# A two-layer graph network on one core: the batch steps of the first layer in groups of their own, and fifteen copied tiles in fourteen groups

## The chip, the cores and the metric

The kernel runs on one core of one Trainium2 chip. The metric is the device time of one execution in microseconds, lower is better. The core has five engines that run side by side: PE (TensorE, matmuls and transposes), DVE (VectorE), ACT (ScalarE), POOL (GpSimd, here the issuer of gathers) and SP (SyncE, the issuer of plain DMAs). Each works through its own instructions in order; a semaphore makes one wait for another.

## The reference

12,500 nodes with 128 features, 200,000 edges sorted by their target `dst`, and 50 features for each edge. Two layers follow each other:

```python
h = relu(layernorm(x))
x = x + segment_sum(h[src], dst) @ W_rel.T + b_rel + h @ W_root.T        # layer 0
h = relu(layernorm(x))
edge = silu(edge_attr_50 @ We1 + be1) @ We2 + be2
agg = segment_sum(h[src] * edge, dst)
x = x + h + silu(agg @ Wn1 + bn1) @ Wn2 + bn2                            # layer 1
```

All of it is in float32.

## The kernel before

**Tiling.** The edges are cut into 196 groups of 1024, each of eight tiles of 128 edges. The nodes are cut into 25 batches of 512 (the last is smaller). For each layer a hand-written loop goes over the groups, and an edge tile goes through three steps: `fetch` gathers the 128 source rows into a buffer `hs` with an indirect DMA that POOL issues; `compare` (DVE) makes a 0/1 matrix `oh` that says which of 128 neighbouring target nodes each edge belongs to; `scatter` (PE, L391) multiplies the two and so sums the rows by target. `add` (DVE, L409) adds the result of a group to the sums of all nodes, which stay on the chip, transposed, in one half of the tensor `both`. There are six `hs` buffers, so POOL may gather up to six groups ahead of `scatter`.

**Layer 0's first 17 groups** normalise the gathered rows of `x` themselves; meanwhile all nodes are normalised once (`node_first`), written to memory as `h0_d`, and kept on the chip, transposed, in the other half of `both` (the table). From group 17 on the rows come from `h0_d`, already normalised.

**Copied tiles.** With all nodes in the table, a tile's rows can also be had without POOL: for each of its 128 edges a column of the table is copied into a tile `hc`, which PE transposes (`turn`, L633) and ACT puts into its place in `hs` (`place`, L639). The columns are shared between DVE (`HC[layer]` of them, L606) and ACT (the rest, L608). Their addresses come from a row of indices, `help_at`, that the engine's sequencer loads into registers (`take`, L591), at most `HL` = 16 at a time. `HELP[layer]` says how many tiles are copied in how many groups: layer 0 has (1, 1), one tile in each group, from group 18 on; layer 1 has (9, 10). A copied tile is the last of its group, and `fetch` leaves it out. `chunks` cuts a tile's columns over the groups that share the work, and `spread` issues those of one group after all else of that group. A tile is wanted `HW` = 4 groups after the group that ends its copying.

**Batch steps.** Edges are sorted, so the sums of a batch of nodes are complete after a known group (`ready[b]`). Then the batch is finished by a list of parts, which `plan` hangs to the groups that follow, one part for each. In layer 0 these are `node_sum` (PE: bias and two products, L471 and L475; then DVE at once: add the old features, L483, and the moments of the layer norm, L289 and L292; then ACT at once: the square root, L294), `node_norm` (DVE: reciprocal and scale, L299 and L301; ACT: the normalised rows, L308), `node_keep` (DVE, L512), `node_store` (SP: `h1_d` and `keep_d` to memory, and the load for the batch four later), `node_turn` (PE, four transposes, L531) and `node_send` (ACT, L537). All use one PSUM bank, `b3`, so that a batch's sum waits for the batch before to be sent. What falls beyond the last group is issued at its end. Layer 1's gathers wait until the last batches of `h1_d` are in memory.

**Order.** In each group of layer 0 the loop issues: the gathers of the next group (POOL), the next `compare` and the `add` of the group before (DVE), `scatter` (PE), then the planned parts of the group, then the columns (DVE and ACT). Engines run ahead of each other only as far as the semaphores let them.

Of the kernel before, what the change touches and what calls it, by code (L numbers as in the profile page):

```python
# [19 lines left out]
P = 128  # L20
D = 128
GT = 8
GE = GT * P
# [4 lines left out]
HB = 6  # L28
# [3 lines left out]
XB = 4  # L32
FB = 4
EP = 51
HELP = ((1, 1), (9, 10))
HC = (60, 56)
HW = 4
TABLE = 16512
HL = 16
# [27 lines left out]
def helped(n_nodes, n_edges):  # L67

    ng = n_edges // GE
    nbt = len(last_groups(n_nodes, n_edges))
    layers = []
    for begin, (tiles, groups) in ((min(ng, -(-nbt // 2) + FB) + 1, HELP[0]), (1, HELP[1])):
        ends = (begin - 1 - -(i + 1) * groups // tiles for i in range(ng * tiles // groups))
        layers.append((begin, [(e + HW, e) for e in ends if e + HW < ng - 1]))
    return layers


# [21 lines left out]
def kernel(  # L102
# [35 lines left out]
    NG = NT // GT  # L138
# [4 lines left out]
    batches = [(b * NB * P, min(NB, -(-(N - b * NB * P) // P))) for b in range(NBT)]  # L143
    FG = min(NG, -(-NBT // 2) + FB)
    places, blocks = help_places(N, n_edges)
    helps = [
        (layer, h, e, begin, j)
        for layer, (begin, groups) in enumerate(helped(N, n_edges))
        for j, (h, e) in enumerate(groups)
    ]  # L150
    helped_groups = {(layer, h) for layer, h, *_ in helps}

    def rows_of(ap, n0, rows, nt):
        return ap[n0 : n0 + rows * nt, :].rearrange("(t p) d -> p t d", p=rows)
# [36 lines left out]
    with (  # L191
# [9 lines left out]
        hs = many(HB, [P, GT, D], "hs")  # L201
# [8 lines left out]
        stn, mvn = many(3, [P, NB, 6], "stn"), many(3, [P, NB, 2], "mvn")  # L210
# [6 lines left out]
        h1 = h0[:2]  # L217
# [16 lines left out]
        def inc(ins, sem, by=1):  # L234

            if sem not in sems:
                sems[sem], counts[sem] = tc.alloc_semaphore(f"s_{sem}"), 0
            ins.then_inc(sems[sem], by)
            counts[sem] += by
            return sem, counts[sem]  # L240

        def at(engine, *needs):

            best = {}
            for need_ in needs:
                if need_ is not None:
                    best[need_[0]] = max(best.get(need_[0], 0), need_[1])
            for sem, n in best.items():
                if n > seen.get((engine.engine, sem), 0):
                    seen[engine.engine, sem] = n  # L250
                    engine.wait_ge(sems[sem], n)
# [4 lines left out]
        def fetch(layer, g):  # L256

            k = layer * NG + g
            at(G, done["src", 0 if g < 8 else 1], done.get(("ap", k - (HB if g < NG - 8 else LB))))
            if layer:  # L260
                at(G, *(done["h1 out", b] for b in range(max(0, NBT - 2), NBT)))
            elif g >= FG:
                at(G, *(done["h0 out", b] for b in range(max(0, NBT - 3), NBT)))
            for t in range(tiles_of[g] - ((layer, g) in helped_groups)):
                ins = G.indirect_dma_start(  # L265
                    out=hs[k % HB][:, t, :], out_offset=None,
                    in_=h1_d if layer else x if g < FG else h0_d,
                    in_offset=bass.IndirectOffsetOnAxis(
                        ap=src_sb[:, g * GT + t : g * GT + t + 1], axis=0
                    ),  # L270
                )
                done["hs", k] = inc(ins, f"hs{k % HB}", 16)
# [9 lines left out]
                ALU.is_equal,  # L282
            )

        def stats(xr, n, rows, st_, mv_, sd_, free):

            at(V, *free)
            for t in range(n):
                ins = V.bn_stats(st_[:rows, t, :], xr[:rows, t, :])  # L289
            at(V, inc(ins, "dve"))  # L290
            for t in range(n):
                ins = V.bn_aggr(mv_[:rows, t, :], st_[:rows, t, :])  # L292
            at(A, inc(ins, "dve"))
            ins = A.activation(sd_[:rows, :n], mv_[:rows, :n, 1], AF.Sqrt, bias=eps[:rows])  # L294
            return inc(ins, "act")

        def scales(n, rows, mv_, sd_, rs_, nm_, deviations):
            at(V, deviations)
            ins = V.reciprocal(rs_[:rows, :n], sd_[:rows, :n])  # L299
            at(V, inc(ins, "dve"))  # L300
            ins = V.scalar_tensor_tensor(  # L301
                nm_[:rows, :n], mv_[:rows, :n, 0], -1.0, rs_[:rows, :n], op0=ALU.mult, op1=ALU.mult
            )
            return inc(ins, "dve")
# [155 lines left out]
        def node_table(b, turned):  # L460
# [3 lines left out]
            ins = A.copy(halves[0][:, n0 : n0 + m], turned.rearrange("p t d -> p (t d)")[:, :m])  # L464
            done["table", b] = inc(ins, "act")

        def node_sum(b):

            n0, nt = batches[b]
            at(T, done.get(("sent", b - 1)), done["const"], done["ones"], done["table", b])  # L470
            T.matmul(op[:, :nt, :], ones_r, b_rel_r[:, :nt, :], start=True, stop=False)  # L471
            for half, w_sb in zip(halves, (w_root_sb, w_rel_sb)):
                for t in range(nt):
                    s = n0 + t * P
                    ins = T.matmul(  # L475
                        op[:, t, :], half[:, s : s + P], w_sb,
                        start=False, stop=(half is agg and t == nt - 1),
                    )
                at(T, done["add", ready[b]])
            done["op", b] = inc(ins, "pe")  # L480
            at(V, done["op", b], done["xt", b])
            o = op[:, :nt, :]
            ins = V.tensor_add(o, o, xt[b % XB][:, :nt, :])  # L483
            done["dev", b] = stats(
                op, nt, P, stn[2], mvn[2], sdn[2], (inc(ins, "dve"), done.get(("h1", b - 1)))
            )
            if b >= cleared:
                at(V, done["op", b], *done.get("columns", ()))
                ins = V.memset(halves[0][:, n0 : n0 + WG], 0.0)
                done["sums", 1].append(inc(ins, "dve"))  # L490

        def clear(b0, b1):
# [3 lines left out]
            ins = A.copy(halves[0][:, s0:s1], zero.to_broadcast([P, s1 - s0]))  # L496
            done["sums", 1].append(inc(ins, "act"))

        def node_norm(b):
            n0, nt = batches[b]  # L500
            at(A, scales(nt, P, mvn[2], sdn[2], rsn[2], nmn[2], done["dev", b]))
            if b < 2:
                at(A, *(done["h0 out", b] for b in range(max(0, NBT - 3), NBT)))
            else:
                at(A, done["h1 out", b - 2], done["keep", b - 2], done["h1 turned", b - 2])
            done["h1", b] = normalized(h1[b % 2], op, nt, P, rsn[2], nmn[2])
# [125 lines left out]
            at(T, done["b3"] if layer else done.get(("placed", i - 2)), done["table", NBT - 1])  # L632
            done["tile", i] = inc(T.transpose(bank, hc[i % 3], ident), "pe")  # L633

        def place(i, layer, h):
            bank = b3[:, :P] if layer else tp[i % 2][:, 0, :]
            k = layer * NG + h
            at(A, done["tile", i], done.get(("ap", k - HB)))
            done["hx", k] = done["placed", i] = inc(A.copy(hs[k % HB][:, GT - 1, :], bank), "act")  # L639
            if layer:  # L640
                done["b3"] = done["placed", i]

        with tc.tile_critical():
# [88 lines left out]
            def plan(layer, g, what):  # L732
                beside[layer].setdefault(min(max(g, 0), NG), []).append(what)

            cleared = NBT
            for layer, parts in (
                (0, (node_sum, node_norm, node_keep, node_store, node_turn, node_send)),
                (1, (node_hidden, node_out, node_out_store)),
            ):
                begin = 0 if layer else FG  # L740
                for b in range(NBT):
                    begin = max(begin, ready[b] + 1)
                    if not layer and begin > NG - 6:
                        cleared = min(cleared, b)
                    for i, part in enumerate(parts):
                        plan(layer, begin + i, lambda b=b, part=part: part(b))
                    begin += len(parts) - 1
            for i in range(4):
                b0, b1 = (cleared * j // 4 for j in (i, i + 1))
                if b0 < b1:  # L750
# [2 lines left out]
                plan(0, -(-NBT // 2) + 1, lambda b=b: node_load(b))  # L753
            for b in range(min(2, NBT)):
                plan(1, ready[0] - 1, lambda b=b: node_load(b, keep_d))
            for i, (layer, h, e, begin, j) in enumerate(helps):
                tiles, groups = HELP[layer]
                for g in range(begin, e + 1):
                    lo, hi = (min(max((g + d - begin) * tiles / groups - j, 0), 1) for d in (0, 1))
                    if lo < hi:  # L760
                        shares.setdefault((layer, g), []).append((i, lo, hi))
                plan(layer, e + 1, lambda i=i, layer=layer: turn(i, layer))
                if not layer:
                    plan(0, e + 2, lambda i=i, h=h: place(i, 0, h))
            placed = {e + 1: (i, 1, h) for i, (layer, h, e, *_) in enumerate(helps) if layer}
            plan(0, FG, check_a)
            plan(0, FG + 1, check_b)
            for g in range(0, min(2 * EG, NG), EG):
# [5 lines left out]
            for layer in range(2):  # L774
# [5 lines left out]
                for g in range(NG):  # L780
# [29 lines left out]
                        what()  # L810
                    spread(layer, g)
                    if layer and g in placed:
                        place(*placed[g])
                add(layer, NG - 1)
                for what in beside[layer].get(NG, ()):
                    what()
# [191 lines left out]
```

## Time and profile before

| | us |
|---|---|
| median of 3 runs (lowest to highest) | 4920.62 (4913.62 to 4926.87) |
| the profiled execution | 4865.67 |
| its span in the profile | 4863.9 |

Busy time by stage, from the windows of the trace:

| stretch, us | what runs | PE | DVE | ACT | POOL | PE clock |
|---|---|---|---|---|---|---|
| 0 to 275 | layer 0 without copied tiles | 94.7 | 120.7 | 133.4 | 177.2 | 0.75 |
| 275 to 2345 | layer 0 with copied tiles | 750.8 | 1129.1 | 1340.6 | 1125.3 | 0.61 |
| 2345 to 2450 | end of layer 0, start of layer 1 | 41.2 | 16.9 | 17.4 | 63.1 | 0.62 |
| 2450 to 4863 | layer 1 | 1668.0 | 1484.1 | 1559.7 | 1263.5 | 0.74 |

The busiest groups of the whole span (the page's fifth part) are POOL's gathers (2648 of 944 ns, 2499.4 us), ACT's column copies at L608 (23,936 of 190 ns, 2596.6 us in all since neighbours overlap), DVE's at L606 (19,840 of 150 ns, 1588.2 us) and PE's products at L391 (1268.7 us). The register loads at L591 take 1025 ns on ACT's sequencer and 1104 ns on DVE's in the median; they are not counted as busy.

How to read it: times are from one execution under the hardware profiler. In the lists of groups, the numbers after the bar are the busy time of the group, the mean of one instruction, and the idle time of the engine just before the group's instructions with what ended it; "issue" is idle time in which the engine waited for nothing that the profile shows, and "remote" one whose releaser is not known. Register, branch and semaphore instructions are not counted as busy.

### The profile page before, as it was taken

The numbers are of one execution on the slowest core, as the hardware profiler recorded it, in microseconds if no ns is written. First come the engines' busy times: TensorE is split into PE (matmuls) and PEld (weight loads), VectorE is DVE, ScalarE is ACT, GpSimd is POOL, SyncE is SP. The second block draws the span as 40 slices with busy tenths as digits, with TensorE's granted clock in tenths as the row PEclk, the third lists the DMA queues.
The fourth block names the chain that finished last, engine by engine and source line by source line (L and its number), as shares of the span: only waits on it lengthen the run. The fifth ranks groups of instructions, "written<-read, shape, count | busy, mean of one in ns | idle before, by whom it ended". The sixth has DMA issues, their size and how long they took to land.

```text
span 4863.9 us, 77667 instructions
## 1 busy us (share of the span) xinstructions
PE 2554.6 (53%) x11440; PEld 1986.8 (41%) x11440; DVE 2750.9 (57%) x21943; ACT 3051.0 (63%) x24975; POOL 2629.1 (54%) x2791
## 2 busy tenths in 40 slices
PE   2433333333333333334456767677666776667777
PEld 1423333332332333333344545455444554444555
DVE  3545555555455555555256566666655665666665
ACT  4646656666666666667356666666666666666664
POOL 6655555555555555554555455555554555555544
PEclk9666655566556666656677777777777777777778
DMA  3411111111111111111122222212221222222221
GB/s 109 112 49 50 51 43 47 47 52 46 44 45 53 45 45 53 47 47 43 52 63 58 59 62 63 59 55 61 64 58 55 59 61 59 63 61 61 58 57 48
DMA packets 187106, 275.72 MB, mean 57 GB/s; under 512 B 48331, under 2 KB 136658, under 8 KB 181586
## 3 DMA queue, kind: packets, MB, share of 16 engines
q0 software_dynamic: 89088, 182.63, 14.5%
q1 hardware_dynamic: 97300, 87.96, 5.9%
q14 instruction: 429, 3.51, 0.2%
q8 instruction: 93, 1.52, 0.1%
q10 hardware_dynamic: 196, 0.09, 0.0%
HBM read 244.89 MB, written 25.60 MB: 56 GB/s over the span
## 4 chain that ended last, share of the span: by engine, by line
ACT 33%; issue 28%; DVE 16%; PE 11%; another core or an unknown queue 8%; ACTq 3%; DVEq 1%; SPq 0%; DMA 0%
ACT hc L608 28%; DVE hc L606 9%; PE bank L391 4%; ACT hid L358 3%; PE pair L355 3%; ACTq L591 3%; DVE oh L278 2%; PE pair L368 2%; DVEq L591 1%; DVE stn L289 1%; ACT hs L639 1%; PE bank L475 1%; DVE st L289 0%; DVE hs L380 0%
## 5 line engine op out<-in xcount | busy, mean ns | idle before, releaser
L265 POOL DMA_INDIRECT hs<-h_d,src_sb x2648 | 2499.4, 944 | 2137.2 <-PE bank L391 1119.3
L608 ACT COPY hc<-both 128x4 uint8 x23936 | 2596.6, 190 | 1364.9 <-issue 1344.9
L606 DVE TENSOR_TENSOR hc<-both,bank 128x4 uint8<-128x4 uint8 x19840 | 1588.2, 150 | 1238.9 <-issue 1226.3
L391 PE MATMUL bank<-oh,hs 128*128 128x128 f32 x6252 | 1268.7, 386 | 291.1 <-issue 120.1
L391 PEld LDWEIGHTS bank<-oh,hs 128*128 128x128 f32 x6252 | 1194.4, 294 | 525.5 <-issue 264.2
L633 PE MATMUL pair<-ident,hc 128*128 128x128 f32 x172 | 73.0, 424 | 1281.1 <-ACT hc L608 411.5
L355 PE MATMUL pair<-ef,we_sb 50*128 50x512 f32 (+1 forms) x782 | 549.8, 837 | 75.8 <-ACT hid L358 33.5
L633 PEld LDWEIGHTS pair<-ident,hc 128*128 128x128 f32 x172 | 30.4, 176 | 1318.9 <-issue 778.5
L278 DVE TENSOR_TENSOR oh<-bank,rel 128x1024 f32<-128x1024 f32 x392 | 475.0, 1212 | 16.9 <-issue 16.7
L376 DVE TENSOR_TENSOR pair<-pair,be_sb 128x1024 f32<-128x1024 f32 x196 | 240.3, 1226 | 407.6 <-PE pair L368 214.9
L368 PE MATMUL pair<-we_sb,hid 128*128 128x128 f32 x3126 | 441.6, 302 | 4.7 <-issue 4.7
L368 PEld LDWEIGHTS pair<-we_sb,hid 128*128 128x128 f32 x3126 | 434.9, 222 | 3.0 <-issue 3.0
L358 ACT ACTIVATE hid<-pair,be_sb 128x1024 f32<-128x1024 f32 x196 | 217.1, 1108 | 105.5 <-remote 58.9
L355 PEld LDWEIGHTS pair<-ef,we_sb 50*128 50x128 f32 x782 | 172.7, 244 | 260.2 <-issue 222.4
L380 DVE TENSOR_TENSOR hs<-pair,hs 128x1024 f32<-128x1024 f32 x196 | 239.3, 1221 | 17.6 <-DMA hs<-h_d,src_sb 8.1
L633 PE MATMUL bank<-ident,hc 128*128 128x128 f32 x170 | 58.6, 345 | 353.6 <-remote 87.1
L633 PEld LDWEIGHTS bank<-ident,hc 128*128 128x128 f32 x170 | 26.2, 154 | 391.6 <-issue 137.9
L265 POOL DMA_INDIRECT hs<-in_x,src_sb x136 | 128.5, 945 | 73.2 <-issue 40.2
L409 DVE TENSOR_TENSOR both<-both,bank 128x128 f32 x392 | 109.0, 278 | 71.8 <-remote 47.1
L483 DVE TENSOR_TENSOR bank<-bank,xt 128x512 f32<-128x512 f32 (+1 forms) x25 | 17.2, 689 | 153.7 <-PE bank L475 52.9
L294 ACT ACTIVATE sdn<-mvn,eps 128x4 f32<-128x4 f32 (+1 forms) x50 | 14.9, 298 | 125.0 <-DVE mvn L292 45.6
L555 PE MATMUL bank<-bn_r,ones_r 1*128 1x512 f32 (+1 forms) x50 | 37.8, 845 | 90.0 <-remote 60.7
(69 smaller groups left out, 888.9 us busy)
## 6 DMA issues: line engine op xcount, KB each, us to landing
hs<-h_d,src_sb POOLq DMA_INDIRECT x2648
ef<-in_ef_t SPq DMA_DIRECT2D x98, 408.0 KB
xt<-in_x SPq DMA_DIRECT2D x48, 256.0 KB
h_d<-h SPq DMA_DIRECT2D x48, 256.0 KB
keep_d<-xt SPq DMA_DIRECT2D x24, 256.0 KB
xt<-keep_d SPq DMA_DIRECT2D x24, 256.0 KB
out_x<-xt SPq DMA_DIRECT2D x24, 256.0 KB
hs<-in_x,src_sb POOLq DMA_INDIRECT x136
```

Of the source, the lines that this page charges most:

```text
L265: ins = G.indirect_dma_start(out=hs[k % HB][:, t, :], out_offset=None, in_=h1_d if layer else x if g < FG else h0_d, in_offset=bass.Indire ...
L278: return V.tensor_tensor(oh[k % OB][:, :n, :], io.unsqueeze(1).to_broadcast([P, n, W]), rel[:, g, :n].unsqueeze(2).to_broadcast([P, n, W]) ...
L355: ins = T.matmul(hp_b[:, c : c + m], we1_sb, e[:, c : c + m], start=True, stop=True)
L358: ins = A.activation(hid[g % 2][:, :n], hp_b[:, :n], AF.Silu, bias=be1_sb)
L368: ins = T.matmul(wp[:, t, :], hid[g % 2][:, t * P : (t + 1) * P], we2_sb, start=True, stop=True)
L376: ins = V.tensor_add(w, w, be2_sb.unsqueeze(1).to_broadcast([P, n, D]))
L380: done["msg", g] = inc(V.tensor_mul(h, w, h), "dve")
L391: ins = T.matmul(ap[k % AB], hs[k % HB][:, t, :], oh[k % OB][:, t, :], start=(t == 0), stop=(t == tiles_of[g] - 1),)
L591: _, columns = nc.values_load_multi_w_load_instructions(help_at[row : row + 1, block, lo:hi], engines=[kind], min_val=TABLE, max_val=TABLE ...
L606: ins = V.tensor_tensor(to, column, zero_b, ALU.bitwise_or)
L608: ins = A.copy(to, column)
L633: done["tile", i] = inc(T.transpose(bank, hc[i % 3], ident), "pe")
```

## The change

It has two parts.

The first takes `node_sum` and `node_norm` of layer 0 apart. `node_sum` keeps the matmuls; the add and the moments become `node_moments` (DVE), the square root `node_deviations` (ACT), reciprocal and scale `node_scales` (DVE), and `node_norm` keeps the normalised rows (ACT). Each of these has a group of its own, so that an engine's part stands a group after the part that it reads. `node_keep`, `node_store` and `node_turn` share the group after `node_norm`, and `node_send` has the next: a batch takes seven groups where it took six. A batch that begins in the last groups (after `NG - 9`) has its nine parts in three groups. The instructions of a batch are the same.

The second changes two sizes for layer 0: `HELP[0]` from (1, 1) to (15, 14), and `HC[0]` from 60 to 56. Fifteen tiles are copied in fourteen groups, so that one group in fourteen has two copied tiles; its second takes the last place but one, which the new `slot` says. DVE copies 56 columns of a tile and ACT 72. A tile's columns no longer begin and end with a group. Layer 1's sizes stay.

```diff
-HELP = ((1, 1), (9, 10))
-HC = (60, 56)
+HELP = ((15, 14), (9, 10))
+HC = (56, 56)
...
-        ends = (begin - 1 - -(i + 1) * groups // tiles for i in range(ng * tiles // groups))
-        layers.append((begin, [(e + HW, e) for e in ends if e + HW < ng - 1]))
+        ends = [begin - 1 - -(i + 1) * groups // tiles for i in range(ng * tiles // groups)]
+        slots = [ends[:i].count(e) for i, e in enumerate(ends)]
+        layers.append((begin, [(e + HW, s, e) for s, e in zip(slots, ends) if e + HW < ng - 1]))
...
-            for t in range(tiles_of[g] - ((layer, g) in helped_groups)):
+            for t in range(tiles_of[g] - helped_groups.count((layer, g))):
...
+        def node_moments(b):
+            n0, nt = batches[b]
             at(V, done["op", b], done["xt", b])
             o = op[:, :nt, :]
             ins = V.tensor_add(o, o, xt[b % XB][:, :nt, :])
-            done["dev", b] = stats(
-                op, nt, P, stn[2], mvn[2], sdn[2], (inc(ins, "dve"), done.get(("h1", b - 1)))
-            )
+            means[b] = moments(op, nt, P, stn[2], mvn[2], (inc(ins, "dve"), done.get(("h1", b - 1))))
...
+        def node_deviations(b):
+            means[b] = deviations(batches[b][1], P, mvn[2], sdn[2], means[b])
+
+        def node_scales(b):
+            means[b] = scales(batches[b][1], P, mvn[2], sdn[2], rsn[2], nmn[2], means[b])
+
         def node_norm(b):
             n0, nt = batches[b]
-            at(A, scales(nt, P, mvn[2], sdn[2], rsn[2], nmn[2], done["dev", b]))
+            at(A, means[b])
...
-            done["hx", k] = done["placed", i] = inc(A.copy(hs[k % HB][:, GT - 1, :], bank), "act")
+            done["hx", k] = done["placed", i] = inc(A.copy(hs[k % HB][:, GT - 1 - slot, :], bank), "act")
...
-                (0, (node_sum, node_norm, node_keep, node_store, node_turn, node_send)),
-                (1, (node_hidden, node_out, node_out_store)),
+                (0, (
+                    (0, node_sum), (1, node_moments), (2, node_deviations), (3, node_scales),
+                    (4, node_norm), (5, node_keep), (5, node_store), (5, node_turn), (6, node_send),
+                )),
+                (1, ((0, node_hidden), (1, node_out), (2, node_out_store))),
...
-                    for i, part in enumerate(parts):
+                    for i, part in parts:
+                        if not layer and begin > NG - 9:
+                            i //= 3
                         plan(layer, begin + i, lambda b=b, part=part: part(b))
-                    begin += len(parts) - 1
+                    begin += i
```

`moments` and `deviations` are the two halves of the old `stats`, which still calls them one after the other for layer 0's first groups.

More of the change, by code (lines that the diff above doesn't have):

```diff
@@ L146 @@
     helps = [
-        (layer, h, e, begin, j)
+        (layer, h, slot, e, begin, j)
         for layer, (begin, groups) in enumerate(helped(N, n_edges))
-        for j, (h, e) in enumerate(groups)
+        for j, (h, slot, e) in enumerate(groups)
     ]
-    helped_groups = {(layer, h) for layer, h, *_ in helps}
+    helped_groups = [(layer, h) for layer, h, *_ in helps]
     def rows_of(ap, n0, rows, nt):
@@ L283, in compare, with moments @@
             )
-        def stats(xr, n, rows, st_, mv_, sd_, free):
+        def moments(xr, n, rows, st_, mv_, free):
             at(V, *free)
@@ L292, in stats, with deviations, scales @@
                 ins = V.bn_aggr(mv_[:rows, t, :], st_[:rows, t, :])
-            at(A, inc(ins, "dve"))
+            return inc(ins, "dve")
+        def deviations(n, rows, mv_, sd_, ready_):
+            at(A, ready_)
             ins = A.activation(sd_[:rows, :n], mv_[:rows, :n, 1], AF.Sqrt, bias=eps[:rows])
             return inc(ins, "act")
-        def scales(n, rows, mv_, sd_, rs_, nm_, deviations):
-            at(V, deviations)
+        def stats(xr, n, rows, st_, mv_, sd_, free):
+            return deviations(n, rows, mv_, sd_, moments(xr, n, rows, st_, mv_, free))
+        def scales(n, rows, mv_, sd_, rs_, nm_, ready_):
+            at(V, ready_)
             ins = V.reciprocal(rs_[:rows, :n], sd_[:rows, :n])
@@ L465, in node_table @@
             done["table", b] = inc(ins, "act")
+        means = {}
         def node_sum(b):
@@ L633, in turn, with place @@
             done["tile", i] = inc(T.transpose(bank, hc[i % 3], ident), "pe")
-        def place(i, layer, h):
+        def place(i):
+            layer, h, slot, *_ = helps[i]
             bank = b3[:, :P] if layer else tp[i % 2][:, 0, :]
@@ L755 @@
                 plan(1, ready[0] - 1, lambda b=b: node_load(b, keep_d))
-            for i, (layer, h, e, begin, j) in enumerate(helps):
+            placed = {}
+            for i, (layer, h, _, e, begin, j) in enumerate(helps):
                 tiles, groups = HELP[layer]
@@ L762 @@
                 plan(layer, e + 1, lambda i=i, layer=layer: turn(i, layer))
-                if not layer:
-                    plan(0, e + 2, lambda i=i, h=h: place(i, 0, h))
-            placed = {e + 1: (i, 1, h) for i, (layer, h, e, *_) in enumerate(helps) if layer}
+                if layer:
+                    placed[e + 1] = i
+                else:
+                    plan(0, e + 2, lambda i=i: place(i))
             plan(0, FG, check_a)
@@ L812 @@
                     if layer and g in placed:
-                        place(*placed[g])
+                        place(placed[g])
                 add(layer, NG - 1)
@@ L969, in by_tile @@
         return np.pad(v, (0, pad), constant_values=fill).reshape(-1, P).T
-    helps = [h for _, groups in helped(a["x"].shape[0], n_edges) for h, _ in groups]
+    helps = [
+        (h + 1) * GT - 1 - slot
+        for _, groups in helped(a["x"].shape[0], n_edges)
+        for h, slot, _ in groups
+    ]
     places, blocks = help_places(a["x"].shape[0], n_edges)
     help_t = np.zeros((P, blocks[-1], P), np.int32)
-    for place, h in zip(places, helps):
-        help_t[place] = a["src"][(h + 1) * GE - P : (h + 1) * GE]
+    for place, t in zip(places, helps):
+        help_t[place] = a["src"][t * P : (t + 1) * P]
     arrays = {
```

## The prediction

> **What bounds the kernel now.** I first read the page's engine row, then asked for the groups, the waits and the timeline of one stretch, 300 to 2280 us. It lies wholly in the part that the change touches: 167 groups of the first layer, all of them helped, in 1980 us, so 11.86 us a group. The order of the later layer is not edited.
>
> ```profile
> PE 2554.6 (53%) x11440; PEld 1986.8 (41%) x11440; DVE 2750.9 (57%) x21943; ACT 3051.0 (63%) x24975; POOL 2629.1 (54%) x2791
> ```
>
> No engine looks full here. The groups of the stretch tell more (busy, mean ns of one | idle before it, by whom it was ended):
>
> ```profile
> L608 ACT COPY hc<-both 128x4 uint8 x11303 | 1223.5, 190 | 619.3 <-issue 609.8
> L265 POOL DMA_INDIRECT hs<-h_d,src_sb x1139 | 1074.3, 943 | 907.2 <-PE bank L391 507.8 <-issue 299.0 <-remote 96.7
> L606 DVE TENSOR_TENSOR hc<-both,bank 128x4 uint8<-128x4 uint8 x9963 | 811.7, 150 | 731.7 <-issue 724.5
> L633 PE MATMUL pair<-ident,hc 128*128 128x128 f32 x166 | 70.4, 424 | 1245.4 <-ACT hc L608 396.5 <-remote 376.6 <-ACT hs L639 339.0
> L483 DVE TENSOR_TENSOR bank<-bank,xt 128x512 f32<-128x512 f32 x21 | 14.7, 700 | 135.1 <-remote 46.5 <-PE bank L475 45.5 <-issue 43.1
> L294 ACT ACTIVATE sdn<-mvn,eps 128x4 f32<-128x4 f32 x21 | 6.2, 297 | 50.4 <-DVE mvn L292 23.6 <-DVE stn L289 22.0 <-issue 4.7
> ```
>
> POOL is not the bound: it idles for PE to free a gather buffer (507.8 us). PE is not either: before the transpose of a copied tile (L633) it waits 1245.4 us, and where a releaser is named it is ACT. That leaves DVE and ACT, which share the copying of columns. The waits of ACT in the stretch:
>
> ```profile
> ACT hc L608 <- issue: 609.8, 1083, 1.2
> ACT sdn L294 <- DVE mvn L292: 23.6, 5, 8.0
> ACT sdn L294 <- DVE stn L289: 22.0, 9, 5.3
> ACT hs L639 <- issue: 11.5, 22, 0.9
> ```
>
> Apart from "issue" (idle with no releaser) ACT waits about 70 us of 1980, 50 of them in the batch step. Column copies account for 1223.5 + 609.8 us. I also paired the ends of each group's columns: in every one of the 172 helped groups ACT ends after DVE, by 5.3 us in the mean, and the transpose starts 0.1 to a few us after ACT's last copy. **ACT sets the pace of this layer**, with DVE close behind.
>
> What the issue gaps are, I read from the timeline around a batch step (start, duration, work, idle before it in brackets):
>
> ```profile
> 1044.87 6.16 ACT L608 COPY hc<-both 128x4 uint8 x61
> ...
> 1054.25 2.07 PE L471 MATMUL bank<-b_rel_r,ones_r 1*128 1x512 f32 x2
> 1054.62 0.29 ACT L608 COPY hc<-both 128x4 uint8 x2 [1.06 <-issue]
> ...
> 1056.06 0.38 ACT L608 COPY hc<-both 128x4 uint8 x3 [0.52 <-issue]
> ...
> 1058.12 1.91 PE L475 MATMUL bank<-w_rel_sb,both 128*128 128x128 f32 x8
> ...
> 1058.92 3.96 ACT L608 COPY hc<-both 128x4 uint8 x36 [0.52 <-issue]
> 1062.72 0.70 DVE L483 TENSOR_TENSOR bank<-bank,xt 128x512 f32<-128x512 f32 x1 [8.30 <-remote]
> ```
>
> Sixty-one copies run without a gap in 6.16 us (101 ns each); ten us later two or three go per 0.7 us; then 36 flow again. The windows show what differs: no DMA share in 1044.9 to 1050, 0.21 in 1053.5 to 1058.9. Binning all ACT work of the stretch by whether gather packets are moving gives 4.5 instructions a us while they are (1382 us) and 9.0 while not (598 us). So the gaps belong to the gathers, not to a partner that ACT waits for. A gather costs about 1382/1139 = 1.2 us of half speed, and what does not fit beside it is done between gathers.
>
> **The change part by part.**
>
> *Tiles.* The helped tiles of layer 0 rise from 172 to 184. POOL loses 12 gathers. POOL has idle time, so its own 12 x 1.25 us (0.944 busy plus 0.30 to the next) buy nothing; the half speed that they cause does: 12 x 1.2 x 0.5 = **-7 us** (ends 0 and -15).
>
> *Columns.* ACT copied 68 of 128 columns per tile, now 72: 184 x 72 - 172 x 68 = **1552 more copies**, 77 a group for 68. DVE: 184 x 56 - 172 x 60 = -16, nothing. Price of an ACT copy: from below 95.7 ns, the mean step between starts where they follow each other closely (149 us); from above 1833.3/11303 = 162 ns, gaps included (252 us). Nearer is the gap-free row, 101 ns: no gather is added, so the extra copies fall between gathers: **+157 us**.
>
> *Register loads.* A tile's columns now straddle groups, so chunks of 16 break more often: I count 121 more loads on ACT (860 to 981), 97 more on DVE (688 to 785). On ACT a load hides behind queued copies: the gaps that end at one total 46 us over about 816, **+7 us** (ends 0 and 34, if each shows the 0.28 us of the visible ones). On DVE some 0.35 us each, +34 us, under ACT's longer time.
>
> *Placing.* 12 more copies of L639 at 257 ns, **+3 us** on ACT. The 12 transposes on PE (0.42 us) lie in PE's idle time, as do those twice in a group.
>
> *Batch steps.* DVE's 135.1 us at L483 go: its add comes a group (11.9 us) after the matmuls, which in the timeline take from 1054.25 to 1060.03. But DVE is not last; this time turns into slack. ACT's 50.4 us at L294 and some 5 before L308 go too, since the square root now finds moments a group old. Of these, 30 us lie beside moving gathers, where ACT runs at half speed anyway: I take **-40 us** (ends -20 and -55).
> What is late next: nothing on ACT but its own copies. PE's four transposes (node_turn) now stand in the same group as DVE's node_keep and wait for it; behind them on PE are the helped transpose and the next scatter. DVE's lead of 5.3 us over ACT covers that wait. If DVE lost the lead, it would cost a few us in each of 25 batches. On SP the two stores and the load of four batches later move two groups; that load is needed 30 groups on. POOL's queue is only shortened.
>
> *End of the layer.* The last two batches are squeezed into three and one groups. Their chain (L483, norm, keep, transposes, send, next sum: 2365 to 2382) follows data, not group numbers; I allow 0 (ends -10 and +5).
>
> Sum on ACT: 157 + 7 + 3 - 40 - 7 = **+120 us**; ends 149 + 3 - 55 - 15 - 10 = +72 and 252 + 34 + 3 - 20 + 5 = +274.
>
> **One rule weighed.** The row: in the stretch ACT is busy 1289.8 of 1980 us, 65%. The Trainium skill (Perfetto Trace Analysis, Identifying the Most-Contended Engine) says that for Scalar the occupancy is a fair measure of how close it is to its limit. By that, a third of ACT would be free, 690 us, which would swallow 170 us of copies and loads, and the sum would be the stalls alone, a gain. By the waits, only 70 us of those 690 are waits for anybody. The same page (Optimization Strategy) sends the reader to the semaphores behind the gaps; here there are none. I take the row: ACT is full.
>
> **Rivals.**
> 1. *The gaps are slack, and the stalls were the price.* If copies fit into the 610 us of issue idle, ACT's extra work is free, and DVE's 135 us decide: -135 + 34 (loads) = about -100, some of it left to ACT: -60 to -100, so 4820 to 4860. For it: DVE stands up to 11 us at a time, and groups around a batch are the longest. Against: ACT ends last in every group. 0.10.
> 2. *Cancel out.* Half the copies fit, within 15 us of before. 0.05.
> 3. *The mean price decides.* The extra copies meet gathers like the old ones and cost 162 ns, with visible loads: +200 to +270, 5120 to 5190. For it: gathers restart as soon as a buffer is free. Against: their number falls. 0.13.
> 4. *The text moves less than it says.* The instruction lists show 25,488 ACT copies for 23,936 and 12 gathers fewer, so I give it nothing.
>
> **The numbers.** The profiled execution took 4865.67 us (span 4863.9); plus 120 is 4986, +2.5%. The runs' median, 4920.62, lies 55 us above that execution; the same 120 on it give **5041**. The main case (0.72) reaches 4990 to 5120. With part of the third rival the range is 4985 to 5150. About 0.3% (15 us) is what a measurement here can tell from no change. Faster: 0.10; within: 0.05; slower: 0.85.
>
> **What would show it.** ACT copies of L608 up by 1552 at an unchanged 190 ns, and the helped stretch longer by about 0.7 us a group; no idle left at L483, under 10 us at L294; POOL's idle for PE larger, not smaller; ACT's lead-in to the transpose still last, with DVE ahead by more than 5.3 us. Wrong if L608's issue idle falls by 100 us or more while the count rises: then the gaps were slack.

## The result and the profile after

The changed kernel takes 5044.19 us in the median (5031.5 to 5047.05, 4 runs), the kernel before beside it 4917.29 (4913.62 to 4926.87, 4 runs): ratio 1.025, interval 1.0226 to 1.0274, so +111 to +135 us. The forecast was 5041, slower. The ratios and intervals here and below are taken over fast runs alone, since a few executions fell into a slower state, and can differ a little from the quotient of the medians beside them.

The spans of the two profiled executions differ by more, 5042.5 and 4863.9 us. I split both at ACT's last column copy of layer 0 and its first of layer 1. From 275 us to the end of layer 0's copies the time goes from 2068 to 2202 us (+134), the passage to layer 1 from 107 to 111, and layer 1, whose order is not edited, from 2413 to 2454 (+41). Layer 1 took 2454 to 2476 us in the profiles of e1 to e4, e11 and e12 as well (below), so it is the profiled execution of before that had a quick layer 1: most of the 50 us by which it lay below its median. The change's part is the +134.

The engine row of the page after:

```profile
PE 2601.5 (52%) x11452; PEld 2013.7 (40%) x11452; DVE 2754.2 (55%) x21927; ACT 3210.4 (64%) x26539; POOL 2617.7 (52%) x2779
```

ACT has 1564 instructions more: 1552 copies and 12 placings. The groups of the same stretch as before, 300 to 2280 us (L626 is the old L608, L624 the old L606, L497 the old L483, L299 the old L294; L308 and L530 are DVE's reciprocal and keep, the old L299 and L512):

```profile
L626 ACT COPY hc<-both 128x4 uint8 x11876 | 1279.3, 190 | 631.6 <-issue 623.0
L267 POOL DMA_INDIRECT hs<-h_d,src_sb x1071 | 1010.1, 943 | 970.2 <-PE bank L400 547.5 <-issue 295.7 <-remote 95.7
...
L651 PE MATMUL pair<-ident,hc 128*128 128x128 f32 x166 | 71.4, 430 | 1131.3 <-ACT hc L626 589.9 <-remote 193.9 <-DVE hc L624 155.1
...
L530 DVE TENSOR_TENSOR xt<-bank,h 128x512 f32<-128x512 f32 x21 | 14.5, 689 | 62.5 <-ACT h L317 57.5 <-ACT hs L658 5.0
L497 DVE TENSOR_TENSOR bank<-bank,xt 128x512 f32<-128x512 f32 x20 | 14.0, 698 | 71.6 <-PE bank L486 24.3 <-PE pair L651 19.1 <-remote 17.7
...
L299 ACT ACTIVATE sdn<-mvn,eps 128x4 f32<-128x4 f32 x20 | 5.9, 293 | 0.5 <-issue 0.5
L308 DVE RECIPROCAL rsn<-sdn 128x4 f32<-128x4 f32 x21 | 3.7, 176 | 122.0 <-ACT sdn L299 107.6 <-ACT hs L658 8.2 <-remote 6.2
```

At the reciprocal and the keep the kernel before had no idle time at all:

```profile
L512 DVE TENSOR_TENSOR xt<-bank,h 128x512 f32<-128x512 f32 x22 | 15.0, 680 | 0.0
...
L299 DVE RECIPROCAL rsn<-sdn 128x4 f32<-128x4 f32 x21 | 3.5, 167 | 0.0
```

ACT's wait for DVE at the square root is gone (50.4 to 0.5 us). DVE stands longer than before: 71.6 + 122.0 + 62.5 us at three places of the batch step, for 135.1 at one, and at the two new places the releaser is ACT by name. POOL waits more for buffers (507.8 to 547.5 us). In 96% of the tiles ACT ends its columns after DVE, by 14.5 us in the mean (5.3 before).

### The profile page after: what moved, and what is told of

The parts are those of the page before. It is cut to its first block, busy times and chain, and to the rows that moved or that the text cites. A ratio compares the mean times of both kernels' runs of the same rounds, so it can differ in the third digit from the quotient of the medians.

```text
span 5042.5 us, 79420 instructions
## 1 busy us (share of the span) xinstructions
PE 2601.5 (52%) x11452; PEld 2013.7 (40%) x11452; DVE 2754.2 (55%) x21927; ACT 3210.4 (64%) x26539; POOL 2617.7 (52%) x2779
## 4 chain that ended last, share of the span: by engine, by line
ACT 50%; issue 27%; PE 7%; another core or an unknown queue 7%; DVE 4%; ACTq 4%; DVEq 0%; SPq 0%; DMA 0%
ACT hc L626 44%; ACTq L609 4%; ACT hid L367 3%; PE pair L364 2%; PE bank L400 2%; PE pair L377 2%; ACT hs L658 1%; DVE hc L624 1%; ACT h L317 1%; DVE oh L280 1%; DVE st L291 1%; DVE stn L291 0%; PE bank L563 0%; DVE hs L389 0%
## 5 line engine op out<-in xcount | busy, mean ns | idle before, releaser
L626 ACT COPY hc<-both 128x4 uint8 x25488 | 2761.6, 190 | 1473.5 <-issue 1456.1
L624 DVE TENSOR_TENSOR hc<-both,bank 128x4 uint8<-128x4 uint8 x19824 | 1588.8, 150 | 1280.9 <-issue 1250.2
L364 PE MATMUL pair<-ef,we_sb 50*128 50x512 f32 (+1 forms) x782 | 566.5, 861 | 107.7 <-ACT hid L367 58.9
L308 DVE RECIPROCAL rsn<-sdn 128x4 f32<-128x4 f32 (+1 forms) x50 | 8.0, 160 | 133.9 <-ACT sdn L299 119.0
L563 PE MATMUL bank<-both,wn_sb 128*128 128x512 f32 (+1 forms) x50 | 36.6, 823 | 83.0 <-remote 38.1
```

The costliest lines, as they stand in the source:

```text
L364: ins = T.matmul(hp_b[:, c : c + m], we1_sb, e[:, c : c + m], start=True, stop=True)
L624: ins = V.tensor_tensor(to, column, zero_b, ALU.bitwise_or)
L626: ins = A.copy(to, column)
```

## The experiments

The runs were made on four chips, here A to D; each is compared with the kernel before on its own chip. Of the kernel before there is one profile, the first, which belongs to the result.

| kernel | chip | this, us | before, us | ratio (interval) |
|---|---|---|---|---|
| e1_split | A | 4924.3 | 4920.2 | 1.0002 (0.9988 to 1.0017) |
| e2_copies | A | 5070.5 | 4920.2 | 1.0311 (1.0278 to 1.0345) |
| e3_split_hc64 | A | 4896.9 | 4920.2 | 0.9946 (0.9924 to 0.9967) |
| e4_hc60 | A | 4981.7 | 4920.2 | 1.0125 (1.0091 to 1.0158) |
| e5_half | B | 3622.6 | 3516.5 | 1.0301 (1.0283 to 1.0318) |
| e6_none | B | 3731.0 | 3516.5 | 1.0607 (1.0589 to 1.0624) |
| e7_six | B | 3419.2 | 3516.5 | 0.9727 (0.9710 to 0.9743) |
| e8_repeat | B | 3515.9 | 3516.5 | 0.9998 (0.9989 to 1.0006) |
| e9_change_again | C | 4930.5 | 4861.8 | 1.0170 (1.0115 to 1.0225) |
| e10_repeat_again | C | 4888.6 | 4861.8 | 1.0063 (1.0042 to 1.0083) |
| e11_loads | D | 4925.8 | 4920.7 | 1.0019 (1.0004 to 1.0034) |
| e12_hc56 | D | 4980.8 | 4920.7 | 1.0096 (1.0060 to 1.0131) |

**The step order alone (e1).** The changed kernel with the old sizes.

```diff
-HELP = ((15, 14), (9, 10))
-HC = (56, 56)
+HELP = ((1, 1), (9, 10))
+HC = (60, 56)
```

> The new step order alone, sizes as before (172 tiles, DVE 60 and ACT 68 columns). If ACT sets the pace of layer 0, only ACT's own waits come back: -40 us (-20 to -57), ratio to before 0.992, and DVE's idle stays but moves to other lines. If DVE's 135 us of standing were the price (first rival): about -100 us, 0.980. If the step order is worth nothing: 1.000.

Neither theory: +1 us, within -6 and +8. The groups of its stretch show what became of the waits:

```profile
L626 ACT COPY hc<-both 128x4 uint8 x11210 | 1220.5, 190 | 661.3 <-issue 652.3
...
L624 DVE TENSOR_TENSOR hc<-both,bank 128x4 uint8<-128x4 uint8 x9998 | 826.0, 155 | 783.9 <-issue 777.2 <-PE bank L400 0.5
...
L530 DVE TENSOR_TENSOR xt<-bank,h 128x512 f32<-128x512 f32 x22 | 15.2, 689 | 10.9 <-issue 5.4 <-remote 2.9 <-ACT hs L658 2.2
L497 DVE TENSOR_TENSOR bank<-bank,xt 128x512 f32<-128x512 f32 x21 | 14.7, 698 | 49.0 <-remote 23.1 <-PE bank L486 12.3 <-issue 10.9
...
L299 ACT ACTIVATE sdn<-mvn,eps 128x4 f32<-128x4 f32 x21 | 6.2, 294 | 3.6 <-issue 3.6
L308 DVE RECIPROCAL rsn<-sdn 128x4 f32<-128x4 f32 x22 | 3.9, 176 | 17.3 <-remote 9.3 <-ACT hs L658 6.7 <-ACT sdn L299 1.4
```

DVE's standing falls from 135.1 us at one place to 77.2 at three (49.0 + 17.3 + 10.9) and ACT's from 50.4 to 3.6, yet the time stays. ACT's issue idle at its copies is 652.3 where the first profile has 609.8: about what the waits had taken seems to have come back as gaps, as if the waits had lain where ACT would have stood anyway. The two profiles are from different chips, and e11, with the old order and loads cut shorter, has 650.3 us of issue idle beside 30.4 us at the square root. So it is shown that removing the waits won nothing, and only argued where the time went.

**The sizes alone (e2).** The changed kernel's code with the batch steps in the groups of before.

```diff
-                    (0, node_sum), (1, node_moments), (2, node_deviations), (3, node_scales),
-                    (4, node_norm), (5, node_keep), (5, node_store), (5, node_turn), (6, node_send),
+                    (0, node_sum), (0, node_moments), (0, node_deviations), (1, node_scales),
+                    (1, node_norm), (2, node_keep), (3, node_store), (4, node_turn), (5, node_send),
...
-                        if not layer and begin > NG - 9:
-                            i //= 3
```

> The new sizes alone (184 tiles, DVE 56 and ACT 72 columns of a tile), batch steps in the order of before. ACT full and 101 ns a copy: +157 +7 +3 -7 = +160 us, ratio 1.033. Copies free in the issue gaps: within 10 us of before, 1.000. Mean price of 162 ns: +250 us, 1.051.

+150 us by the medians, for 160 expected. The cost of the change is in its sizes.

```profile
L497 DVE TENSOR_TENSOR bank<-bank,xt 128x512 f32<-128x512 f32 x20 | 14.0, 700 | 287.0 <-remote 133.5 <-PE bank L486 125.8 <-PE pair L651 16.0
...
L299 ACT ACTIVATE sdn<-mvn,eps 128x4 f32<-128x4 f32 x20 | 5.9, 294 | 26.1 <-DVE mvn L294 16.5 <-issue 5.1 <-DVE stn L291 4.5
```

DVE's standing at L497 is 287.0 us here, twice that of before, while ACT's wait at L299 is 26.1: more ACT work makes DVE wait, not the other way. With these sizes the step order is then worth something: 1.0311 falls to 1.025 with it, some 30 us, with an uncertainty of 20, since the two ratios come from separate comparisons.

**Columns from ACT to DVE (e3, e4).** e3 is the new step order with `HELP[0] = (1, 1)` and `HC[0] = 64`; e4 the changed kernel with `HC[0] = 60`.

> The new step order, one tile in each group, but DVE copies 64 and ACT 64 columns (688 copies moved from ACT to DVE). ACT full: 688 x 0.101 = 69 us less than the step order alone, so about -110 us against before, 0.978, as long as DVE's 48 us of added columns fit under its lead. If DVE were the bound: 48 us more than the step order alone, about +10 us or more.

> The changed kernel (15 tiles in 14 groups, new step order) with DVE at 60 and ACT at 68 columns of a tile: 736 ACT copies and 61 register loads fewer than in the changed kernel, 736 DVE copies more. ACT full: 75 us below the changed kernel, about 4970, ratio to before 1.010. Copies free: no change from the changed kernel, 1.025. DVE the bound: slower than the changed kernel by up to 50 us.

e4 came 62 us below the changed kernel (1.025, from the first comparison, to 1.0125; uncertain by 20) for 75 expected. Against e1, which has the same order and the same 60 and 68 columns, e4 has just the twelve tiles more, and it takes 60 us more (1.0002 to 1.0125 on the same chip, uncertain by 18). So the two sizes share the price about evenly: the 736 columns moved to ACT cost some 84 ns each, the 816 ACT copies of the twelve tiles some 73, loads and placing included. e3 gained 27 us for 110, because the bound changed sides:

```profile
L624 DVE TENSOR_TENSOR hc<-both,bank 128x4 uint8<-128x4 uint8 x10671 | 871.5, 155 | 808.9 <-issue 803.2
...
L651 PE MATMUL pair<-ident,hc 128*128 128x128 f32 x167 | 72.7, 435 | 901.8 <-DVE both L418 430.2 <-DVE hc L624 358.0 <-issue 90.2
```

The transpose now waits for DVE by name, and DVE ends its columns after ACT in all but 1 of 172 tiles, by 8.2 us in the mean; in e1 ACT had ended last in 94% of them, by 8.4. Four columns of a tile, well under 1 us of either engine's work, turned the lead over by 16.6 us, so the size of a lead is no measure of room. DVE's waits measure it better: 77.2 us in e1's stretch, while its copies there take 160 ns each with their gaps ((826.0 + 777.2)/9998, the row L624 of e1), so that 688 more ask for an estimated 110 us. The forecast had counted 48. The slack between the two engines was a few columns wide. e3 is also the one version with all its work done that came out below the kernel before on a chip with gaps, by half a per cent.

**Fewer tiles, fewer gathers, more copies (e5 to e8).** e5 and e6 are the new step order with `HELP[0]` at (1, 2) and (0, 1), so 86 tiles and none, and `HC[0]` at 60. e7 and e8 are the kernel before with one line changed:

```diff
-            for t in range(tiles_of[g] - ((layer, g) in helped_groups)):
+            for t in range(tiles_of[g] - ((layer, g) in helped_groups) * (1 + (not layer))):
```

```diff
                 else:
+                    if not helps[i][0] and c < HC[0] + 9:
+                        A.copy(spare[i % 3][:, 4 * (c - HC[0]) : 4 * (c - HC[0]) + 4], column)
                     ins = A.copy(to, column)
```

> New step order, but only one tile in every two groups is copied (86 tiles; DVE 60 and ACT 68 columns of each). ACT full: 5848 ACT copies fewer than with one in each group, so ACT drops out as the bound; POOL would be next with 7.5 gathers of 1.25 us, 9.4 us a group for 12.0: about -400 us, 4520, ratio 0.92. If copying a tile pays for itself because gathers slow everything: slower than before.

> New step order, no tile copied in layer 0; layer 1 as before. POOL alone sets the pace with 8 gathers of 1.25 us, 10 us a group for 12.0: about -330 us, 4590, ratio 0.93; slower than the half. If gathers were dearer than their 1.25 us: slower than before.

> The kernel before, except that each helped group of layer 0 leaves out one more gather (its seventh tile is multiplied with old rows, so the sums of layer 0 and all that follows are not the reference's). 172 gathers fewer, copies as before. If ACT's issue gaps belong to the gathers (half speed for 1.2 us each): -90 to -103 us, ratio 0.98, and ACT's issue idle in the stretch falls from 610 to about 520 us. If the gaps have another cause: within 10 us of before.

> The kernel before, with 9 of ACT's 68 columns of each tile in layer 0 copied a second time into a spare tile: 1548 ACT copies more, nothing else. ACT full: +156 us at 101 ns a copy, ratio 1.032, like the new sizes alone. If the price of the new sizes lay in the straddled tiles (loads, two tiles in a group) and not in the copies: below +40 us, 1.008.

On chip B the kernel before takes 3516 us, not 4920, and everything turns round. 86 gathers more cost 106.2 us (1.23 each), 172 cost 214.6 (1.25 each), 172 fewer save 97.2 (0.57 each), and 1548 copies more cost nothing. (e5 and e6 also have the new step order; at 1.23 to 1.25 us a gather, the distance at which POOL issues them, nothing is left for it.) In e7, which leaves out a gather that its sums need, POOL begins to wait for buffers again, so that its gathers alone no longer set the pace; ACT and DVE end their columns about 1 us apart there:

```profile
L265 POOL DMA_INDIRECT hs<-h_d,src_sb x954 | 900.0, 943 | 399.4 <-issue 272.2 <-PE bank L391 127.2
```

The groups of e8, 300 to 1600 us (L611 is ACT's copy, L266 the gather, L610 the second copy, L636 the transpose), and its timeline:

```profile
L611 ACT COPY hc<-both 128x4 uint8 x10142 | 1121.7, 190 | 8.5 <-issue 3.5
L266 POOL DMA_INDIRECT hs<-h_d,src_sb x1042 | 983.2, 944 | 317.6 <-issue 311.2 <-PE pair L636 2.4 <-PE bank L392 1.8
...
L610 ACT COPY spare<-both 128x4 uint8 x1341 | 254.7, 193 | 12.7 <-issue 12.4
...
L636 PE MATMUL pair<-ident,hc 128*128 128x128 f32 x150 | 62.2, 415 | 560.8 <-ACT hc L611 526.2 <-DVE hc L607 28.7 <-DVE xt L513 5.6
```

```profile
1004.84 6.02 ACT L611 COPY hc<-both 128x4 uint8 x60
1005.44 0.95 POOL L266 DMA_INDIRECT hs<-h_d,src_sb  x1 [0.30 <-issue]
...
1006.69 0.94 POOL L266 DMA_INDIRECT hs<-h_d,src_sb  x1 [0.30 <-issue]
...
1007.94 0.95 POOL L266 DMA_INDIRECT hs<-h_d,src_sb  x1 [0.30 <-issue]
```

Sixty copies run without a gap beside three gathers, and POOL hardly ever waits for a buffer (about 6 of 1300 us): it issues every 1.25 us and sets the pace. It does so although ACT still ends its columns after DVE in all 172 tiles, by 3.3 us in the mean, and although the transpose waits for ACT by name. The issue idle of ACT's copies is 3.5 us, where the first profile had 609.8. So the gaps of the other chips are not made by gathers alone: the same gathers, closer together, make none here. The prediction rested its price on the reading that the gaps belong to the gathers, and as a cause gathers do not suffice; that gaps and gathers coincide remains true of the first chip. What e5 to e7, with many tiles or gathers fewer, would do on a chip with gaps was not measured.

**The change and the second copies again (e9, e10).** The changed kernel and e8's kernel, on another chip.

> The changed kernel once more, beside the kernel before on whatever chip this lands on. Where the kernel before takes about 4920 us: 1.025 again. Where it takes about 3516 us and has no issue gaps, POOL's gathers set the pace and ACT's copies are free: 12 gathers of 1.25 us saved, 15 us, ratio 0.996 (0.993 to 1.000). If ACT were still the bound there: 1.03.

> The kernel before with 1548 ACT copies made twice, nothing else (as e8_repeat). Where the kernel before takes about 4920 us, ACT is full: +156 us, ratio 1.032. If there the price of the new sizes lay in straddled tiles and loads and not in the copies: below 1.008. Where it takes about 3516 us: 1.000 again.

Chip C is of the kind with gaps. The change costs +83 us by the ratio (56 to 109) and 69 by the medians, so less surely than in the first comparison. But the 1548 second copies cost 31 (20 to 40), 20 ns each and not 101. The stretch of e10:

```profile
L611 ACT COPY hc<-both 128x4 uint8 x10942 | 1260.5, 189 | 421.7 <-issue 414.1
...
L610 ACT COPY spare<-both 128x4 uint8 x1446 | 275.1, 191 | 138.6 <-issue 136.7
```

and that of e9:

```profile
L626 ACT COPY hc<-both 128x4 uint8 x12095 | 1296.1, 190 | 614.8 <-issue 605.5
```

The issue idle of e10's two lines, 551 us, is less than e9's 605.5 with about as many copies in all; the same kernel had 16 us of 1300 on chip B (e8). Gaps over 0.1 us stand before 18% of the second copies, 15% of the copies right behind them and 6% of the rest, so these nine columns lie where gaps are commonest; in the first profile too, gaps stand before 18% of ACT's first nine columns of a tile and 9% of the others. This suggests that part of the gaps can hold added copies, as the first rival had it, though not the change's own; no profile of the kernel before on chip C shows it.

**Loads and moved columns (e11, e12).** To part the change's price: the kernel before with loads of at most 12 columns in layer 0, and the kernel before with `HC = (56, 56)`.

```diff
-                for c in range(lo, hi, HL):
-                    yield i, c, min(c + HL, hi)
+                step = HL if layer else 12
+                for c in range(lo, hi, step):
+                    yield i, c, min(c + step, hi)
```

> The kernel before, with register loads of at most 12 columns for 16 in layer 0: the same copies, but 172 loads more on ACT and 172 more on DVE (the change adds 121 and 97). On a chip where the kernel before takes 4860 to 4920 us: if loads are hidden as predicted, +10 to +20 us, ratio 1.003; if the change's price lay in its 218 loads (0.4 to 0.6 us each), +140 to +210 us, 1.03 to 1.04. On a chip of 3516 us: 1.000.

> The kernel before, with DVE at 56 and ACT at 72 columns of a tile in layer 0: 688 copies moved from DVE to ACT, loads, tiles and gathers as before. On a chip of 4860 to 4920 us: ACT the slowest at 101 ns a copy, +69 us, ratio 1.014; at the price that the twice-made copies showed (19 ns), +13 us, 1.003. On a chip of 3516 us: 1.000.

344 loads more cost 9 us (2 to 17), so the change's 218 are not its price. 688 copies moved from DVE to ACT cost 47 us (30 to 64; 60 by the medians), 69 ns each, without a tile, load or gather changed; DVE's wait at L483 is 333.8 us, for 135.1 in the first profile and 130.8 in e11 on the same chip:

```profile
L608 ACT COPY hc<-both 128x4 uint8 x11366 | 1232.1, 190 | 642.6 <-issue 633.3
...
L483 DVE TENSOR_TENSOR bank<-bank,xt 128x512 f32<-128x512 f32 x20 | 14.0, 700 | 333.8 <-remote 236.4 <-PE bank L475 76.0 <-issue 21.4
```

ACT is the later engine on chip D too (in all 172 tiles of e12, by 11.8 us in the mean), and its share of the columns is what counts.

## Why the prediction was right

**ACT sets the pace: right** on A and D by experiment, and by the profiles on the chip of the result and on C. ACT work added made it slower (e2, e12), taken away made it faster until DVE was last (e3, e4). It is a statement about those chips; on B the gathers set the pace, and ACT, busy 1190.8 of 1300 us in e8, had room for 1548 copies. Two readings on the way were loose. Of the 70 us that ACT is said to wait, 48.1 are waits for a named engine; the rest is issue idle at other lines. And DVE's lead of 5.3 us was taken as room for its added loads and waits; e3 shows that the room was far smaller.

**The copies, +157, with loads, placing and gathers +160: right in sum**, 150 measured on A in the old step order; in the new one about 122. The loads were as small as said (e11). The price of 101 ns for any ACT copy is not general: 69 to 84 for columns moved from DVE (e12, e4), some 73 for those of added tiles (e4), some 20 for columns copied twice (e10). All lie below the 162 of the third rival. I have no run that says why a second copy is so much cheaper than a new column.

**The batch steps, -40: too large.** At the old sizes they are worth nothing (e1), at the new ones about 30 us. The waits did go, all but 0.5 us at the square root; that was taken for time won, and at the old sizes none was. The step that failed is the split of the 50 us into 30 beside gathers, counted at half, and 20 free: nearly all was covered. That the time came back as issue gaps is the likely reading of e1, not a shown one.

**"No idle left at L483": wrong in place.** 71.6 us stayed, and 184.5 came up at the reciprocal and the keep, where DVE waits for ACT directly. That DVE's standing is no price was right: in e1 it fell by 58 us and nothing was won.

**The end of the layer, 0:** 107 to 111 us.

**The gaps belong to the gathers: not by themselves** (chip B). No run takes away gathers alone on a chip with gaps, so their part there stays open. The split into 1382 us at 4.5 instructions a us and 598 at 9.0 also counts the pauses between packets as moving: packet by packet, gathers move in 625 us of the stretch, at 4.9, against 6.3 in the rest. The -7 us that hung on it is too small to show. On chip B each gather left out is worth 0.57 to 1.25 us, so that there the change's 12 would save 7 to 15 us; the change was not run on that chip, and this stays an estimate.

**The rule.** The Trainium skill (Perfetto Trace Analysis, Identifying the Most-Contended Engine) takes occupancy as a fair measure for Scalar of how close it is to its roofline. It misled both ways here: at 65% busy ACT had little room (e2, e12), at 92% (1190.8 of 1300 us) added copies were free (e8). Who is waited for is not enough either, since the transpose waits for ACT by name in both (396.5 and 526.2 us). What held in both was to ask which engine hardly waits for another: ACT in the first profile, POOL in e8.

**The total** came within 3 us of the forecast partly by luck, since two errors cancelled. Counted by way of e2, the sizes cost 10 us less than forecast and the step order saved 10 less; by way of e1, the step order saved nothing, 40 less, and the sizes cost about 122 (1.0002 to 1.025), 38 less.

## What to carry to other kernels

Where two engines share a job, look which ends it last in every round: that, not busy time, says which side may take more. How far it ends last does not say how much more: here four columns turned a lead of 8.4 us into a lag of 8.2. And being last of the two does not make it the bound: on chip B ACT was last in every tile, and yet its added copies were free, because POOL, which waited for nobody, set the pace. A wait that is removed is only won if the engine works in its place: compare the idle time that the profile gives to nobody before and after, on one chip. Before paying for one resource with another, measure on more than one chip: here the same program is bound by ACT and DVE on most of them and by POOL on one.

## What the runs showed of the hardware that was not expected

The same kernel takes 3516 us on one chip and 4862 to 4921 on the others, at a granted clock of 0.755 in the median and 0.67 to 0.68. In layer 0 the difference shows as gaps in ACT's and DVE's streams without any releaser, 610 and 725 us of the first profile's stretch (register loads included), during which both let one to three instructions go about every 0.7 us, often at the same instants: 62% of ACT's gaps end within 50 ns of one of DVE's. Single instructions take as long on chip B: an ACT copy 190 ns in both, PE's product 402 ns in the first profile and 404 in e8. Gather packets of 4096 bytes take as long on chip B (246 ns in the mean) as in the first profile (244), so slower transfers are not it. Packets that carry instructions overlap fewer than one in ten of ACT's 1083 gaps. The cause is open. Each chip was used in one session, so what belongs to the chip and what to its state at the time is not told apart.
